# Projecting v for two groups of heads at once in a transformer layer on one core

## The chip, the core and the metric

The kernel runs on one core of a Trainium2 chip. A core has a matrix engine (TensorE, PE in the profile), a vector engine (VectorE, DVE), an engine for activations (ScalarE, ACT), a general one (GpSimd, POOL) and one that here only issues DMAs (SyncE, SP). They run their own instruction streams, each in order, and wait for each other by semaphores. The metric is device time in microseconds (us) of one execution. Before the change it is 2662.03 us in the median of three runs (2661.37 to 2664.33).

## What is computed

The input x has 8 batches of 1024 rows with 512 features. The reference, cut to its core:

```python
qkv = einsum('bte,fe->btf', layernorm(x), in_proj_weight).reshape(b, t, 3, 16, 32)
q, k, v = heads of qkv                      # 16 heads of 32 features
attn = softmax(causal(q @ k.T / sqrt(32)))  # per batch and head
x = x + (attn @ v) @ out_proj_weight.T
z = layernorm(x)                            # and then, over the 8 batches in order:
c = sigmoid(z@wf.T + c@uf.T + bf) * c + sigmoid(z@wi.T + c@ui.T + bi) * tanh(z@wc.T + c@uc.T + bc)
out = x + tanh(z @ wo.T + c_final @ uo.T + bo)
```

The recurrence runs over the batches, with 1024 rows at each step.

## The kernel before

**Numbers.** Matrices are split into two fp16 parts, a high and a low one, and a product is taken as three products of parts (high-high, high-low, low-high). A product over 512 features is therefore 3 x 4 = 12 matmuls into one PSUM buffer. The helper `three` (line 534) issues them with 512 moving columns each; all its matmuls stand under line 539 in the profile, told apart by their tiles.

**Groups.** The 16 heads of a batch are worked on in 4 groups of 4 heads, 32 groups over all batches; `s_` counts them, `b` is the batch and `g` the group in it. `proj(s_)` (line 547) projects a group:

- It loads three weight tiles (q, k, v; each 128 partitions x 2 parts x 4 x 128, 256 KB) from a DRAM tensor SQ. Their ring `wg` has three slots, which lie side by side in the raw tile wxr (so the profile calls them wxr). A ring hands out any free slot, and its users take their turn in order of creation (fifo).
- q and k: for each half of the 1024 rows, 12 matmuls with the weights stationary and 512 rows of zT (the normalized input, transposed) moving, into a buffer of the ring pj (two PSUM buffers). The moving operand is `zt()[:, :, c, k]`, four stretches of 128 columns that lie 2 KB apart. ScalarE (L570) and VectorE (L571) evict the high and low part into a tile `nat`, and a DMA writes it to DRAM (QK).
- v: here the rows are stationary and the weights move. For each half and each of its four blocks of 128 rows, 12 matmuls of 128 columns (line 586) write a quarter of one pj buffer. ScalarE (L591) and VectorE (L592) evict it, 128x512, into the one tile of ring `vs`, and a DMA writes that to DRAM (VD), 264 KB.

`stack_load` (line 600) later loads the stacked q and k into `stk` (three slots) and v into `vt`. `a_group` (line 637) computes scores for the row maxima in the PSUM buffer sa, `m_rows` (line 681) turns the maxima round with one matmul into sa (line 690) and copies them out on VectorE (line 692). `b_group` (line 759) and, from the 21st pair of heads on, `turned_rows` (line 729) compute scores again, exponentiate, split (GpSimd, line 757) and multiply by v (line 721). `out_proj` (line 855) projects the result; `recur` (line 882) runs the recurrence, with weights wf loaded from SF through a ring of two slots, and `csplit` (line 872) splits its state (lines 877 and 878).

**Order.** Nothing is issued by loops at run time. Every step is an operation with an engine, an estimated duration and a due time `at`; `Plan.schedule` (line 107) makes one fixed order from them before the program is built. At each step it takes the engine whose next operation can start earliest and, of those that can start at that moment, the one with the least due time. It counts with estimated durations (0.68 us for 12 matmuls of 128 columns), with ring slots that come free, and for a DMA with SP's time to issue it (0.32 us; 3.5 us for a transposing one), 270 GB/s on one common channel, and 2.2 us more to land. What comes out is each engine's instruction stream; on the chip an instruction that isn't ready holds up all behind it on its engine, SP's DMAs included.

Due times count in steps: one group has 65 (18 x TAU / 9 with TAU = 32.5). From a group's start, q is due at 0 and 5, k at 10 and 15, v at 20 and 25. On the chip a batch took 298 us around the middle of the run.

Of the kernel before, what the change touches and what calls it, by code (L numbers as in the profile page):

```python
# [10 lines left out]
F16 = mybir.dt.float16  # L11
# [23 lines left out]
class Ring:  # L35

    def __init__(self, tiles, fifo=True, over=()):
        self.tiles, self.fifo, self.over = tiles, fifo, over  # L40
        self.free = [(0.0, i) for i in range(len(tiles))]
        self.queue = deque()
        self.left, self.end = 0, 0.0

    def buf(self):
        return Buf(self)


class Buf:
    def __init__(self, ring=None, tile=None):  # L50
        self.ring, self.tile, self.slot = ring, tile, None
        self.left, self.end, self.acc = 0, 0.0, []
        self.view = None
        if ring is not None:
            ring.left += 1
            if ring.fifo:
                ring.queue.append(self)
# [19 lines left out]
class Plan:  # L77
# [29 lines left out]
    def schedule(self):  # L107
        avail = {e: [] for e in LATENCY}
        clock = {e: 0.0 for e in LATENCY}
        dma = 0.0  # L110

        shared = 0.0

        def enter(o):
            avail[o.eng].append(o)
            for e in o.alt:
                avail[e].append(o)

        for o in self.ops:
            o.n = len(o.pre)  # L120
            o.ready = 0.0
            for p in o.pre:
                p.succ.append(o)
            if not o.n:
                enter(o)
        left = len(self.ops)
        while left:
            best = None
            for e, l in avail.items():
                t = clock[e]  # L130
                pick = None
                for o in l:
                    s = o.ready if o.ready > t else t
                    if o.alt:

                        f = {x: max(o.ready, clock[x]) + y + SPARE.get(x, 0.0) for x, y in (*o.alt.items(), (o.eng, o.dur))}
                        if min(f.values()) < f[e]:
                            continue
                    if o.port and shared > s:
                        s = shared  # L140
                    if pick is not None and s > pick[0]:
                        continue
                    ok = True
                    for b in o.bufs:
                        if b.ring is not None and b.slot is None:
                            q = b.ring
                            if not q.free or (q.fifo and q.queue[0] is not b) or any(x.left for x in q.over):
                                ok = False
                                break
                            f = max([min(q.free)[0]] + [x.end for x in q.over])  # L150
                            if f > s:
                                s = f
                    if ok:
                        k = (s, o.at, o.seq)
                        if pick is None or k < pick[:3]:
                            pick = (*k, o)
                if pick is not None and (best is None or pick[0] < best[0]):
                    best = (*pick, e)
            assert best is not None, "the plan has no next operation"
            s, _, _, o, e = best  # L160
            avail[o.eng].remove(o)
            for x in o.alt:
                avail[x].remove(o)
            if e != o.eng:
                o.eng, o.dur = e, o.alt[e]
            for b in o.bufs:
                if b.ring is not None and b.slot is None:
                    x = min(b.ring.free)
                    b.ring.free.remove(x)
                    b.slot = x[1]  # L170
                    if b.ring.fifo:
                        b.ring.queue.popleft()
            o.start, o.end = s, s + o.dur
            clock[o.eng] = o.end
            if o.port:
                shared = o.end
            done = o.end + LATENCY[o.eng]
            if o.size is not None:
                dma = max(dma, o.end) + o.size / DMA_RATE
                done = dma + DMA_LATENCY  # L180
            for b in o.bufs:
                b.left -= 1
                b.end = max(b.end, done)
                if b.ring is not None and not b.left:
                    b.ring.free.append((b.end, b.slot))
                    b.ring.left -= 1
                    b.ring.end = max(b.ring.end, b.end)
            for x in o.succ:
                x.n -= 1
                x.ready = max(x.ready, o.end if x.eng == o.eng and o.size is None else done)  # L190
                if not x.n:
                    enter(x)
            left -= 1
        return sorted(self.ops, key=lambda o: (o.start, o.seq))
# [3 lines left out]
def layer(ctx, tc, x_in, wqkvT, woT, ffn, woffT, uoffT, vecs, bo, inc, out):  # L198
# [142 lines left out]
    def new(tag):  # L341
        return R[tag].buf()

    def dma(dst, src, at, r=(), w=(), size=256.0, hold=(), dur=0.32, transpose=False, after=(), e="SP"):

        if transpose:
            fn = lambda: sp.dma_start(dst(), src(), transpose=True)
        else:
            fn = lambda: eng[e].dma_start(dst(), src())
        return op(e, dur, fn, r, w, at, size * 1024.0, hold, after)  # L350
# [192 lines left out]


    wgs, QK, VD = {}, {}, {}

    def proj(s_):
        b, g = divmod(s_, G)
        at0 = t_a(18 * s_) - 1.7 * TAU - X_SH * max(0.0, 1 - s_ / X_RAMP) if s_ else -280.0
        for which in range(3):  # L550
            if (s_, which) not in wgs:
                w = wgs[s_, which] = new("wg")
                dma(w, lambda which=which: SQ()[g, which], at0 - 10.0 + 2 * PSTEP * which, r=[(SQ, (g, which))], w=[w])
        w = [wgs.pop((s_, i)) for i in range(3)]
        qk = QK[s_] = new("QK")
        vd = VD[s_] = new("VD")
        at = at0
        for which in range(2):
            t = new("nat")
            for half in range(2):  # L560
                if s_ == 0:
                    at = -250.0 + 60.0 * half
                zt, p = zT[b, half], new("pj")
                three(p, p, lambda c, k, zt=zt: zt()[:, :, c, k], lambda a, k, which=which: w[which]()[:, a, k], 512,
                      lambda k: [zt, w[which]], at)
                cols = slice(half * 512, half * 512 + 512)
                scale = 2.0 ** (-21 - which)
                hi = lambda t=t, cols=cols, which=which: t()[:, 1 - which, cols]
                lo = lambda t=t, cols=cols, which=which: t()[:, which, cols]
                op("ACT", 0.6, lambda p=p, hi=hi, scale=scale: act.activation(hi(), p(), AF.Copy, scale=scale), [p], [(t, (half, 0))], at)  # L570
                op("DVE", 0.7, lambda p=p, hi=hi, lo=lo, scale=scale: dve.scalar_tensor_tensor(lo(), p(), scale, hi(), ALU.mult, ALU.subtract),  # L571
                   [p, (t, (half, 0))], [(t, (half, 1))], at)
                at += PSTEP
            dma(lambda which=which: qk()[2 * which : 2 * which + 2].rearrange("w p t -> p w t"), t, at,
                r=[(t, (i, j)) for i in range(2) for j in range(2)], w=[(qk, which)], size=512)
        if s_ == 0:
            at = -100.0
        for half in range(2):
            v = new("vs")
            zt, p = zT[b, half], new("pj")  # L580
            for n in range(4):
                def fn(n=n, zt=zt, p=p):
                    i = 0
                    for k in range(KE):
                        for a, c in ((0, 0), (0, 1), (1, 0)):
                            pe.matmul(p()[:, n * 128 : n * 128 + 128], zt()[:, n, a, k], w[2]()[:, c, k], start=i == 0, stop=i == 3 * KE - 1)  # L586
                            i += 1
                op("PE", 0.68, fn, [(zt, n // 2) if b else (zt, (n // 2, n % 2)), w[2]], [p], at)
            src = lambda p=p: p().rearrange("p (n h d) -> p n h d", n=4, d=D)
            dst = v  # L590
            op("ACT", 0.6, lambda src=src, dst=dst: act.activation(dst()[:, :, :, 32:64], src(), AF.Copy, scale=2.0 ** -21), [p], [(v, 0)], at)  # L591
# [1 line left out]
               [p, (v, 0)], [(v, 1)], at)  # L593
            at += PSTEP
            dma(lambda half=half: vd()[:, half * 4 : half * 4 + 4], v, at, r=[(v, 0), (v, 1)], w=[(vd, half)], size=270)


    stk, vt, ms, MX = {}, {}, {}, {}

    def stack_load(P):  # L600
# [8 lines left out]
                at, r=[(qk, 0), (qk, 1)], w=[(t, j)])  # L609
        if p == 0:  # L610
            v = vt[s_] = new("vt")
            dma(v, VD[s_], t_b(9 * P) - 0.3 * TAU, r=[(VD[s_], 0), (VD[s_], 1)], w=[v], size=540)


    MASKED = 22
# [629 lines left out]
```

## Time and profile before

| | |
|---|---|
| median of three runs | 2662.03 us (2661.37 to 2664.33) |
| the profiled execution's own time | 2666.67 us |
| its span, first to last instruction | 2665.0 us |
| granted TensorE clock, mean | 0.996 |
| DMA moved | 477.99 MB, mean 179 GB/s |
| v projection, line 586 | 3072 matmuls, 219 ns for one (median) |
| its evictions, lines 591 and 592 | 597 and 686 ns for one (medians in batches five to eight) |
| weight tiles loaded from SQ | 93 DMAs, 3.3 us to landing (median) |
| v written to DRAM (VD<-vs) | 64 DMAs, 2.6 us to landing (median) |

How to read what follows. A row of the order of time has the start and the duration in us, engine, line, operation, tiles written <- read, shapes, and a count of like instructions merged; in brackets idle time of the engine before it and what ended it. The duration of one matmul holds its latency, and matmuls are pipelined, so what a matmul costs in a stream is read from the start of one row to the start of the next. A row of waits has the engine and line that waited, who was waited for, us in total, times, and the longest. "SPq" is SP's queue of DMA issues.

### The profile page before, as it was taken

The page shows a single profiled execution, that of the slowest core. Times are in us where ns is not written, and L with a number is a line of the kernel's source. Part 1 is how long each engine was busy: PE and PEld are TensorE (multiplying, and loading weights), DVE is VectorE, ACT ScalarE, POOL GpSimd, SP SyncE. Part 2 cuts the span into 40 slices and gives each one's busy share as a digit, 9 for nine tenths or more (in the row PEclk, how much of TensorE's full clock was granted, in tenths as well). Part 3 has the DMA queues.
Part 4 walks back from the last instruction along what each step waited for, and adds up shares of the span by engine and source line. Part 5 has one row for each costly group of instructions (what it writes and reads, how often), then busy time and mean ns, then how long its engine had stood idle before and what let it go on. Part 6 is the DMA issues. An engine that isn't in the chain of part 4 may idle for free.

```text
span 2665.0 us, 61520 instructions
## 1 busy us (share of the span) xinstructions
PE 2619.7 (98%) x24622; PEld 1512.8 (57%) x24636; DVE 1799.4 (68%) x4252; ACT 1836.3 (69%) x2290; POOL 1561.7 (59%) x1171
## 2 busy tenths in 40 slices
PE   8999999999999999999999999999999999999999
PEld 5666655666555555555555555555555555544444
DVE  5888777777677676767767676767776676422455
ACT  4688879888877777776777677777776777522222
POOL 3576777678667666666767666666766676400000
PEclk9999999999999999999999999999999999999999
DMA  6666676568567686687758686687756775564565
GB/s 228 172 194 196 157 185 173 147 173 217 134 148 187 187 203 164 171 201 177 195 148 191 182 207 165 171 195 193 185 145 161 187 172 128 148 205 150 197 223 211
DMA packets 526992, 477.99 MB, mean 179 GB/s; under 512 B 393841, under 2 KB 393841, under 8 KB 523121
## 3 DMA queue, kind: packets, MB, share of 16 engines
q1 hardware_dynamic: 526704, 474.06, 67.7%
q8 instruction: 193, 3.16, 0.5%
q14 instruction: 95, 0.77, 0.1%
HBM read 270.54 MB, written 108.53 MB: 142 GB/s over the span
## 4 chain that ended last, share of the span: by engine, by line
PE 87%; DVE 3%; DMA 2%; issue 1%; ACT 1%; POOL 0%; SPq 0%; DVEq 0%; ACTq 0%; POOLq 0%
PE pj L539 45%; PE av L721 9%; PE pt L539 8%; PE sb L779 7%; PE sa L665 7%; PE pj L586 5%; PE av L539 3%; PE sb L738 1%; DVE m L673 1%; DMA wf<-SF 1%; DVE cs L878 1%; PE sb L781 1%; PE sa L667 1%; DMA stkr<-mt 0%; ACT er L784 0%
## 5 line engine op out<-in xcount | busy, mean ns | idle before, releaser
L757 POOL TENSOR_TENSOR Pr<-er,Pr 128x1024 f16<-128x1024 f32 x569 | 1216.0, 2142 | 425.2 <-ACT Pr L756 330.8
L784 ACT ACTIVATE er<-sb,ebias,usc 128x1024 f32<-128x1024 f32 x488 | 586.2, 1201 | 175.2 <-PE sb L779 124.8
L539 PEld LDWEIGHTS <-wf 128*128 128x128 f16 x4320 | 401.3, 97 | 424.4 <-DMA wf<-SF 3.3
L756 ACT ACTIVATE Pr<-er 128x1024 f16<-128x1024 f32 x576 | 603.2, 1054 | 28.0 <-POOL er L793 17.5
L675 DVE CUSTOM_DVE_ANT_0 sa<-sa,tri 128x896 f32<-128x896 f32 (+3 forms) x588 | 409.8, 697 | 177.6 <-PE sa L665 167.1
L539 PE MATMUL pj<-z2T,wf 128*128 128x512 f16 x2016 | 497.6, 378 | 0.0
L539 PE MATMUL pj<-cs,wf 128*128 128x512 f16 x1728 | 419.8, 379 | 0.0
L721 PEld LDWEIGHTS <-Pr 128*128 128x128 f16 x9792 | 333.0, 96 | 84.5 <-issue 1.9
L539 PE MATMUL pj<-zT,wxr 128*128 128x512 f16 x1536 | 378.9, 380 | 0.2
L721 PE MATMUL av<-vt,Pr 128*128 128x65 f16 (+2 forms) x9792 | 348.5, 183 | 1.5 <-POOL Pr L757 0.9
L665 PE MATMUL sa<-stkr 96*128 96x512 f16 (+3 forms) x1348 | 299.2, 319 | 18.1 <-DVE m L673 10.2
L779 PE MATMUL sb<-stkr 98*128 98x128 f16 (+3 forms) x1624 | 308.6, 294 | 4.5 <-ACT er L784 2.4
L673 DVE TENSOR_REDUCE m<-sa 128x1 f32<-128x256 f32 (+7 forms) x340 | 241.3, 746 | 83.8 <-PE sa L667 83.1
L539 PEld LDWEIGHTS <-wxr 128*128 128x128 f16 x1728 | 158.8, 97 | 162.0 <-issue 2.6
L793 POOL TENSOR_SCALAR_AFFINE_SELECT er<-er 128x256 f32<-128x256 f32 (+1 forms) x336 | 122.1, 381 | 171.8 <-ACT er L784 169.1
L779 PEld LDWEIGHTS <-stkr 98*128 98x128 f16 x1624 | 143.1, 97 | 93.4 <-issue 3.6
L586 PE MATMUL pj<-wxr,zT 128*128 128x128 f16 x3072 | 194.2, 219 | 0.6 <-DVE C L911 0.6
L665 PEld LDWEIGHTS <-stkr 96*128 96x128 f16 x1360 | 120.7, 97 | 121.6 <-issue 22.9
L586 PEld LDWEIGHTS <-zT 128*128 128x128 f16 x3072 | 177.6, 98 | 11.1 <-issue 0.9
L539 PE MATMUL pj<-wo,aT 128*128 128x512 f16 x768 | 174.2, 379 | 0.2 <-DVE stkr L865 0.2
L459 POOL TENSOR_TENSOR zsr<-z,zsr 128x512 f16<-128x512 f32 x120 | 138.5, 1158 | 57.4 <-ACT zsr L458 55.5
L747 ACT ACTIVATE er<-sb,m,usc 128x1024 f32<-128x1024 f32 x88 | 105.8, 1202 | 82.0 <-DVE m L744 60.4
(186 smaller groups left out, 2888.7 us busy)
## 6 DMA issues: line engine op xcount, KB each, us to landing
wf<-SF SPq DMA_DIRECT2D x192, 512.0 KB, 3.9
stkr<-QK SPq DMA_DIRECT2D x192, 256.0 KB, 4.5
QK<-natr SPq DMA_DIRECT2D x64, 512.0 KB, 3.9
wxr<-x SPq DMA_DIRECT2D x112, 256.0 KB, 4.1
wxr<-SQ SPq DMA_DIRECT2D x93, 256.0 KB, 3.3
VD<-vs SPq DMA_DIRECT2D x64, 264.0 KB, 2.6
vt<-VD SPq DMA_DIRECT2D x32, 528.0 KB, 4.0
stkr<-X SPq DMA_DIRECT2D x16, 1024.0 KB, 7.3
```

Of the source, the lines that this page charges most:

```text
L459: o = op("DVE", 0.85, lambda: eng[o.eng].tensor_tensor(zs()[:, i, 1], z(), zs()[:, i, 0], ALU.subtract), [z, (zs, (i, 0))], [(zs, (i, 1))] ...
L539: pe.matmul(pv(), sv(a, k), mv_(b, k), start=first and k == 0 and i == 0, stop=last and k == KE - 1 and i == 2)
L586: pe.matmul(p()[:, n * 128 : n * 128 + 128], zt()[:, n, a, k], w[2]()[:, c, k], start=i == 0, stop=i == 3 * KE - 1)
L665: pe.matmul(pp()[:, lo:hi], q[:, h, qb * 128 : qb * 128 + 128], k[:, h, lo - off : hi - off], start=True, stop=not last, skip_group_check= ...
L673: dve.tensor_reduce(m()[:, h, qb : qb + 1], pp()[:, off : off + w], AX.X, ALU.max)
L675: dve.tensor_tensor_reduce(pp()[:, off : off + w], pp()[:, off : off + w], tri[:, T - w :], 1.0, NEG, ALU.add, ALU.max, m()[:, h, qb : qb ...
L721: pe.matmul(av()[:, o + z : o + z + y - x], stat(hl), v()[:, kb, i, x:y], start=c == 1, stop=c == total, skip_group_check=True)
L756: op("ACT", 1.06, lambda: act.activation(W()[:, 0], e(), AF.Copy), [e], [(W, 0)], at)
L757: lo = op("POOL", 2.18, lambda: eng[lo.eng].tensor_tensor(W()[:, 1], e(), W()[:, 0], ALU.subtract), [e, (W, 0)], [(W, 1)], at, alt={"DVE": ...
L779: pe.matmul(pp()[:, off : off + w], k[:, h, kb * 128 : kb * 128 + 128], q[:, h, qb0 * 128 : qb0 * 128 + w], start=True, stop=not last, ski ...
L784: op("ACT", 1.2, lambda: act.activation(e(), pp(), AF.Exp, bias=ebias, scale=TS), [pp, *s("TS")], [e], at)
L793: pool.affine_select(out=x, in_=x, pattern=[[0, n], [1, 128]], compare_op=ALU.is_ge, fill=0.0, base=0, channel_multiplier=-1)
```

## The change

From the fifth batch on (`TWO = 4`), v is projected only in even groups, for that group and the next together:

- An even group loads q's weights into slot 0 of `wg`, v's weights of its own and of the next group into slots 1 and 2, and k's weights into slot 0 again, once q's matmuls have freed it. An odd group loads q into slot 1 and k into slot 2. The slot wanted stands in a new field `want`, and the planner gives a buffer no other slot.
- `values` projects v: for a block of 128 rows, 12 matmuls with 256 moving columns (128 of each group, two stretches that lie 2 KB apart, read from slots 1 and 2 by one access pattern). Two blocks fill one pj buffer. Eviction by ScalarE and VectorE is of 128x512, as before. Two DMAs of half the size write one group's part each to DRAM.
- The four buffers of v in an even group are due at 20, 32, 44 and 56 from the group's start (`VSTEP = 12`). An odd group has q and k alone.

The first four batches, the attention, the recurrence and the end are as before. The diff, cut to its core:

```diff
+    def open(self, b):
+        return [f for f in self.free if b.want is None or f[1] == b.want]
...
-        self.view = None
+        self.view = self.want = None
...
-                            if not q.free or (q.fifo and q.queue[0] is not b) or any(x.left for x in q.over):
+                            free = q.open(b)
+                            if not free or (q.fifo and q.queue[0] is not b) or any(x.left for x in q.over):
...
+    VSTEP, VLATE = 12, 0
+    TWO = 4
...
-        for which in range(3):
+        two = b >= TWO and g % 2 == 0
+        loads = [(g, i) for i in range(3)] if b < TWO else [(g, 0), (g, 2), (g + 1, 2), (g, 1)] if two else [(g, 0), (g, 1)]
+        w = {}
+        for i, (gg, which) in enumerate(loads):
             if (s_, which) not in wgs:
-                w = wgs[s_, which] = new("wg")
-                dma(w, lambda which=which: SQ()[g, which], at0 - 10.0 + 2 * PSTEP * which, r=[(SQ, (g, which))], w=[w])
-        w = [wgs.pop((s_, i)) for i in range(3)]
+                x = new("wg")
+                if b >= TWO:
+                    x.want = (i if two else i + 1) % 3
+                dma(x, lambda gg=gg, which=which: SQ()[gg, which], at0 - 10.0 + 2 * PSTEP * min(i, 2), r=[(SQ, (gg, which))], w=[x])
+            else:
+                x = wgs.pop((s_, which))
+            w[which, gg] = x
...
+        if b >= TWO:
+            for half in range(2 if two else 0):
+                for m in range(2):
+                    values(s_, half, m, [w[2, g], w[2, g + 1]], at + VLATE)
+                    at += VSTEP
+            return
...
+    def values(s_, half, m, w, at):
+
+        v = new("vs")
+        zt, p = zT[s_ // G, half], new("pj")
+        for j in range(2):
+            def fn(n=2 * m + j, o=j * 256):
+                assert (w[0].slot, w[1].slot) == (1, 2)
+                ww = raw["wxr"][:, 512:1536].bitcast(F16).rearrange("p (g a k f) -> p g a k f", g=2, a=2, k=KE)
+                i = 0
+                for k in range(KE):
+                    for a, c in ((0, 0), (0, 1), (1, 0)):
+                        pe.matmul(p()[:, o : o + 256].rearrange("p (g f) -> p g f", g=2), zt()[:, n, a, k], ww[:, :, c, k], start=i == 0, stop=i == 3 * KE - 1)
+                        i += 1
+
+            op("PE", 1.32, fn, [(zt, m), *w], [p], at)
...
+        for i in range(2):
+            dma(lambda i=i: VD[s_ + i]()[:, half * 4 + 2 * m : half * 4 + 2 * m + 2].rearrange("p n h c -> p n (h c)"),
+                lambda i=i: v().rearrange("p (n g) h c -> p n g (h c)", g=2)[:, :, i], at + PSTEP, r=[(v, 0), (v, 1)], w=[(VD[s_ + i], (half, m))], size=135)
...
-            dma(v, VD[s_], t_b(9 * P) - 0.3 * TAU, r=[(VD[s_], 0), (VD[s_], 1)], w=[v], size=540)
+            dma(v, VD[s_], t_b(9 * P) - 0.3 * TAU, r=[VD[s_]], w=[v], size=540)
```

More of the change, by code (lines that the diff above doesn't have):

```diff
@@ L146, in schedule @@
                             q = b.ring
-                            if not q.free or (q.fifo and q.queue[0] is not b) or any(x.left for x in q.over):
+                            free = q.open(b)
+                            if not free or (q.fifo and q.queue[0] is not b) or any(x.left for x in q.over):
                                 ok = False
                                 break
-                            f = max([min(q.free)[0]] + [x.end for x in q.over])
+                            f = max([min(free)[0]] + [x.end for x in q.over])
                             if f > s:
@@ L167, in schedule @@
                 if b.ring is not None and b.slot is None:
-                    x = min(b.ring.free)
+                    x = min(b.ring.open(b))
                     b.ring.free.remove(x)
@@ L549, in proj @@
         at0 = t_a(18 * s_) - 1.7 * TAU - X_SH * max(0.0, 1 - s_ / X_RAMP) if s_ else -280.0
-        for which in range(3):
+        two = b >= TWO and g % 2 == 0
+        loads = [(g, i) for i in range(3)] if b < TWO else [(g, 0), (g, 2), (g + 1, 2), (g, 1)] if two else [(g, 0), (g, 1)]
+        w = {}
+        for i, (gg, which) in enumerate(loads):
             if (s_, which) not in wgs:
-                w = wgs[s_, which] = new("wg")
-                dma(w, lambda which=which: SQ()[g, which], at0 - 10.0 + 2 * PSTEP * which, r=[(SQ, (g, which))], w=[w])
-        w = [wgs.pop((s_, i)) for i in range(3)]
+                x = new("wg")
[5 more added lines that the diff above has]
+            w[which, gg] = x
         qk = QK[s_] = new("QK")
-        vd = VD[s_] = new("VD")
+        for i in range(2 if two else 0 if b >= TWO else 1):
+            VD[s_ + i] = new("VD")
+        vd = VD[s_]
         at = at0
@@ L563, in proj @@
                 zt, p = zT[b, half], new("pj")
-                three(p, p, lambda c, k, zt=zt: zt()[:, :, c, k], lambda a, k, which=which: w[which]()[:, a, k], 512,
-                      lambda k: [zt, w[which]], at)
+                three(p, p, lambda c, k, zt=zt: zt()[:, :, c, k], lambda a, k, which=which: w[which, g]()[:, a, k], 512,
+                      lambda k: [zt, w[which, g]], at)
                 cols = slice(half * 512, half * 512 + 512)
@@ L585, in fn @@
                         for a, c in ((0, 0), (0, 1), (1, 0)):
-                            pe.matmul(p()[:, n * 128 : n * 128 + 128], zt()[:, n, a, k], w[2]()[:, c, k], start=i == 0, stop=i == 3 * KE - 1)
+                            pe.matmul(p()[:, n * 128 : n * 128 + 128], zt()[:, n, a, k], w[2, g]()[:, c, k], start=i == 0, stop=i == 3 * KE - 1)
                             i += 1
-                op("PE", 0.68, fn, [(zt, n // 2) if b else (zt, (n // 2, n % 2)), w[2]], [p], at)
+                op("PE", 0.68, fn, [(zt, n // 2) if b else (zt, (n // 2, n % 2)), w[2, g]], [p], at)
             src = lambda p=p: p().rearrange("p (n h d) -> p n h d", n=4, d=D)
@@ L595, in proj @@
             dma(lambda half=half: vd()[:, half * 4 : half * 4 + 4], v, at, r=[(v, 0), (v, 1)], w=[(vd, half)], size=270)
+    def values(s_, half, m, w, at):
[11 more added lines that the diff above has]
+            op("PE", 1.32, fn, [(zt, m), *w], [p], at)
+        src = lambda: p().rearrange("p (n d) -> p n d", d=D)
+        dst = lambda: v().rearrange("p n h c -> p (n h) c")
+        op("ACT", 0.6, lambda: act.activation(dst()[:, :, 32:64], src(), AF.Copy, scale=2.0 ** -21), [p], [(v, 0)], at)
+        op("DVE", 0.7, lambda: dve.scalar_tensor_tensor(dst()[:, :, 0:32], src(), 2.0 ** -21, dst()[:, :, 32:64], ALU.mult, ALU.subtract),
+           [p, (v, 0)], [(v, 1)], at)
+        for i in range(2):
+            dma(lambda i=i: VD[s_ + i]()[:, half * 4 + 2 * m : half * 4 + 2 * m + 2].rearrange("p n h c -> p n (h c)"),
+                lambda i=i: v().rearrange("p (n g) h c -> p n g (h c)", g=2)[:, :, i], at + PSTEP, r=[(v, 0), (v, 1)], w=[(VD[s_ + i], (half, m))], size=135)
     stk, vt, ms, MX = {}, {}, {}, {}
```

## The prediction

> **What bounds the kernel now.** I read the page's table of busy time first, then its slices, then busy time by stretches of 100 us, then the waits of TensorE, then the order of time around the v projection.
>
> ```profile
> PE 2619.7 (98%) x24622; PEld 1512.8 (57%) x24636; DVE 1799.4 (68%) x4252; ACT 1836.3 (69%) x2290; POOL 1561.7 (59%) x1171
> ...
> PEclk9999999999999999999999999999999999999999
> ```
>
> TensorE is busy for 98% of the span at a full granted clock. No other engine comes near it. In busy time by stretches (start and end, length, busy time of PE, then the other engines), the batches that the change touches look like this:
>
> ```profile
> 1400.00:1500.00 100.00, 100.00 (x975) 59.56 (x974) 69.47 (x186) 73.03 (x90) 70.81 (x60) 1.00 0.83 198
> 1500.00:1600.00 100.00, 100.00 (x905) 56.62 (x903) 72.40 (x194) 74.08 (x95) 66.57 (x58) 1.00 0.78 191
> 1600.00:1700.00 100.00, 98.24 (x956) 57.27 (x953) 68.62 (x172) 74.09 (x90) 66.50 (x51) 1.00 0.66 157
> ```
>
> Most stretches have no idle time at all, and one in three lacks 1.76 us. So in this stage the time is the sum of what TensorE streams, plus one small wait a batch. From 1060 to 2200 us, which holds the v projections of the last four batches, TensorE's waits are two rows:
>
> ```profile
> PE sa L665 <- DVE mt L692: 7.0, 4, 1.8
> PE pj L586 <- DVE C L911: 0.6, 1, 0.6
> ```
>
> The change can therefore gain only what it takes from the stream, and these 7.6 us. It can lose whatever makes TensorE wait, because TensorE takes its instructions in a fixed order and nothing can overtake a matmul that waits.
>
> **The matmuls.** The last four batches hold 16 groups of four heads. Each group projects v with 96 matmuls of 128 columns, 1536 in all. The change makes 768 of 256 columns, with the same stationary tiles, each loaded half as often. What one costs is read from where the next row starts, since the duration of one (219 ns) is mostly latency:
>
> ```profile
> 1257.78 2.75 PE L539 MATMUL pj<-zT,wxr 128*128 128x512 f16 x12
> 1260.37 0.60 PE L665 MATMUL sa<-stkr 96*128 96x512 f16 x3
> ...
> 1273.36 2.17 PE L586 MATMUL pj<-wxr,zT 128*128 128x128 f16 x36
> 1275.37 0.60 PE L665 MATMUL sa<-stkr 96*128 96x512 f16 x3
> ```
>
> 36 matmuls of 128 columns take 1275.37 - 1273.36 = 2.01 us, 55.8 ns each. 12 of 512 columns take 1260.37 - 1257.78 = 2.59 us, 215.8 ns each. A straight line through both gives (215.8 - 55.8) / 384 = 0.417 ns a column and 2.4 ns for each matmul whatever its size. So 256 columns cost 55.8 + 128 x 0.417 = 109.2 ns. Two small ones cost 111.6 ns. The saving is 2.4 ns x 768 = **1.9 us**, which is all there is in the stream. The weight load (98 ns for one by itself) is already hidden: the matmuls of 128 columns follow each other in 55.8 ns, on the same line as the large ones, so halving the loads gives nothing.
>
> No matmul of 256 columns stands alone in a long run here, so I bound its cost. From below, half a matmul of 512 columns is 107.9 ns, a saving of 768 x 3.7 = 2.8 us. From above, 111.6 ns, a saving of nothing. A new matmul reads two stretches of 128 columns that lie 2 KB apart. The q and k projections read four stretches of 128 columns at that same step (line 564), and these are the very matmuls that take 215.8 ns, so a slower read is not to be expected. I take 1.9 us, nearest to both rows.
>
> [...]
>
> **The evictions.** Per pair of groups there were four evictions by ScalarE (L591, 597 ns) and four by VectorE (L592, 686 ns), each of 128x512, and there still are four of each. They cost nothing more. The two buffers of PSUM (pj) are taken as often and for as long (24 matmuls of 109.2 ns are 2.6 us, 48 of 55.8 ns were 2.7 us).
>
> **The DMAs.** The weight loads stay at six a pair of groups (four with the even group, two with the odd one). The writes of v to DRAM go from 32 to 64 of half the size; the row of these says 326 ns for an issue, so SP, which issues all DMAs in order, gets 32 x 0.33 = 10 us more in some 1100 us. SP spends most of its time waiting (the waits of its queue begin with 401.6 us behind line 539's matmuls), so I take nothing for it. The one staging tile (vs) is held until both writes land; a landing now takes 2.6 us in the median (2.1 to 5.3 in these batches) and the evictions are planned 12 us apart, so this is covered. Without that cover ScalarE would wait up to some 3 us, and behind it a PSUM buffer.
>
> **The new wait.** In an even group k's weights may only be loaded when q's slot is free. Nothing but q's second half stands between, and in half of these groups k follows q at once. In the 21st group the order of time has q's last three matmuls and k's first six in one unbroken row (counted from the group's start); below it are two rows of SP, and one of the page's table of DMAs (count, size, median us to landing).
>
> ```profile
> 1313.40 2.11 PE L539 MATMUL pj<-zT,wxr 128*128 128x512 f16 x9
> ...
> 1312.51 1.96 SPq L347 DMA_TRANSPOSE Pr<-Pr  x1
> 1316.62 0.35 SPq L349 DMA_DIRECT2D wxr<-SQ  x1
> ...
> wxr<-SQ SPq DMA_DIRECT2D x93, 256.0 KB, 3.3
> ```
>
> The load into that very slot (for the next group, today) was issued at 1316.62, some 2.5 us after q's three (1313.40 + 3 x 0.216 = 1314.05), because SP was behind a transpose; with 3.3 us to landing, k's weights would be there nearly 6 us after q. If k stayed where it is in the order, TensorE would stand for that long with attention and recurrence queued behind it. But the order is not fixed by hand: the planner gives a load 256 KB / 270 GB/s + 2.2 us plus SP's own time, and puts other ready matmuls first. In the odd group q's and k's slots come free only after the last v matmul. By the due times that v is planned at 56 and the next q at 65, and its weights need 2.6 us of matmuls and some 4 us of load, so 2 to 3 us are spare.
>
> How good such planning is can be read from the same kernel. The recurrence's weights (wf<-SF, 192 loads of 512 KB, 3.9 us to landing) also go through a ring of two and are also loaded when a slot is freed. TensorE waited for them three times, 1.8 us in all, and never in the stretch above. So I take 0 for 8 loads of k and 8 pairs of the odd groups, with bounds of 0 and 8 x 3.3 = 26 us (a whole landing for each of k's loads). Against a gain from it speaks that weights never made TensorE wait here.
>
> **The small wait.** The 7.0 us are four waits of 1.76 us, one a batch, at 1080, 1378, 1676 and 1975 us, beside the q projection of the second group:
>
> ```profile
> 1372.86 5.22 DVE L878 SCALAR_TENSOR_TENSOR cs<-C,sig,cs 128x512 f16<-128x512 f32 x2
> 1378.00 0.27 DVE L692 CAST mt<-sa 32x128 f16<-32x128 f32 x1
> ...
> 1378.33 0.59 PE L665 MATMUL sa<-stkr 96*128 96x512 f16 x3 [1.76 <-DVE mt L692]
> ```
>
> VectorE's two operations took 5.22 us in place of twice 0.7 while GpSimd ran; the copy from the score buffer came late, and the next scores with it. It is an accident of alignment, and the change moves 2.6-us blocks of v to just ahead of this place. It may go, stay, or come twice. I take it as unchanged, with bounds of -7.0 us and +7.0 us.
>
> **The sum.** -1.9 (stream) + 0 (weights) + 0 (alignment) = -1.9 us. The profiled execution took 2666.67 us with a span of 2665.0; by the sum it becomes 2664.8. The median of the runs is 2662.03, 4.6 lower, and with the same step it becomes **2660 us**.
>
> **The rivals.**
> 1. The alignment resolves. All four waits of line 665 go: -1.9 - 7.0 = -8.9, 2653 us. For it: batches two to four (480 to 1060 us) show only 0.6 us of waits. Against it: the cause (VectorE behind GpSimd) stays.
> 2. Slower: k's weights come late in the even groups. It decides from (5.3 + 1.9) / 8 = 0.9 us a load on, where the loss leaves the band of 0.2%. For it: SP's order is fixed too, and it was 2.5 us late for this slot; the slowest landing of these tiles was 8.5 us. Against it: the recurrence's loads. With a landing exposed in the four groups where k follows q at once: 4 x 3.3 - 1.9 = +11.3, 2673 us; in all eight, 26.4 - 1.9, 2686 us.
> 3. The change doesn't do what it says: the wide matmul streams no faster than two, 2662 us.
>
> **How the numbers follow.** The likeliest case has 0.55 (own range 2657 to 2667), the first rival 0.2, the second 0.2, the third 0.05. A measurement of this kernel can tell about 0.2%, 5.3 us, from no change: below 2656.7 is faster, above 2667.4 slower. Faster gets the first rival's 0.2, slower the second's 0.2, the same 0.6. The range reaches from just under the first rival, 2652, to just over the second's first price, 2675; what is left out is eight full landings, or waits that pile up at several places.
>
> **What would show it.** In the profile after: 768 matmuls of 256 columns that follow each other in about 109 ns, and 1536 of 128 columns left; TensorE busy about 2 us less. In its waits, line 539 behind a DMA of wxr from SQ would show the second rival, and the row of line 665 behind line 692 missing or doubled decides the first. I am wrong if TensorE's busy time falls by 10 us or more (the loads did count), or if its idle time from 1060 to 2200 us leaves 0 to 15 us.

## The result and the profile after

The changed kernel takes 2684.37 us in the median of five runs (2682.87 to 2687.51), the kernel before 2663.39 us beside it (2661.37 to 2668.21): a ratio of 1.0078, with a 95% interval of 1.0064 to 1.0092. It is **21 us slower**. The prediction said 2660 us, a range up to 2675, and gave slower 2 in 10.

The profiled execution took 2687.51 us with a span of 2685.8. The page's first line on it:

```profile
PE 2628.2 (98%) x23868; PEld 1503.1 (56%) x23868; DVE 1819.6 (68%) x4249; ACT 1834.3 (68%) x2290; POOL 1565.5 (58%) x1174
```

In fewer matmuls TensorE is busy for 8.5 us more, and the span has grown by 20.8. Up to about 940 us both executions keep pace; what differs is the part that the change touches. Busy time in the same kind of stretch as before (the number after the five engines is the granted clock, 0.98 in one of the two and 1.00 in both before):

```profile
1400.00:1500.00 100.00, 97.91 (x809) 53.43 (x808) 66.16 (x179) 71.16 (x90) 68.31 (x58) 0.98 0.72 183
1500.00:1600.00 100.00, 99.38 (x872) 56.61 (x869) 72.89 (x188) 71.47 (x91) 65.99 (x58) 1.00 0.73 193
```

Before, two stretches in three had no idle time at all; now each has some. The four largest rows of TensorE's waits from 980 to 2260 us name what it lacks (three more have 1.3 us together):

```profile
PE pj L544 <- DVE C L966: 12.4, 13, 2.1
PE av L768 <- POOL Pr L804: 2.7, 2, 1.7
PE pj L544 <- DVE natr L588: 1.6, 4, 0.4
PE pj L544 <- DVE C L958: 1.3, 3, 0.4
```

(Lines have moved. Matmuls: 544 is the old 539, 712 the old 665, 737 the old 690, 768 the old 721, 785 the old 738, 631 the new v. On VectorE: 958 is the old 911, 965 and 966 are the old 918 and 919, 588 the old 571. On GpSimd: 804 is the old 757.) Twenty waits, 15.3 us, are for a buffer of `pj`: a matmul waits for VectorE to empty one of the two PSUM buffers that projections, recurrence and output projection share. Before, the same stretch had one such row, 0.6 us. The 7.0 us of line 665 behind line 692 are gone, and no wait is for weights from SQ. The longest of these waits, in order of time, TensorE first and then VectorE:

```profile
1444.15 0.81 PE L544 MATMUL pj<-zT,wxr 128*128 128x512 f16 x3
...
1445.68 0.60 PE L768 MATMUL av<-vt,Pr 128*128 128x65 f16 x16
1448.36 1.10 PE L544 MATMUL pj<-z2T,wf 128*128 128x512 f16 x3 [2.09 <-DVE C L966]
1449.25 1.06 PE L785 MATMUL sb<-stkr 96*128 96x512 f16 x2
...
1446.85 0.73 DVE L965 SCALAR_TENSOR_TENSOR pj<-pj,g 128x512 f32<-128x512 f32 x1
1447.61 0.69 DVE L966 SCALAR_TENSOR_TENSOR C<-pj,C 128x512 f32<-128x512 f32 x1
1448.22 0.68 DVE L588 SCALAR_TENSOR_TENSOR natr<-pj,natr 128x512 f16<-128x512 f32 x1
```

One buffer holds a recurrence unit, the other the first half of q, which the new order has taken early: nine of its twelve matmuls ran from 1433.08 on, the last three only at 1444.15, so it holds its buffer for nearly 16 us, until 1448.90. VectorE empties both only from 1446.85 on. For 2.09 us TensorE takes up no matmul. What follows is slow: the two matmuls of 512 columns from 1449.25 to 1450.10 take 0.43 us each in place of 0.216. In busy time by stretches:

```profile
1440.00:1448.30 8.30, 6.27 (x65) 3.78 (x64) 6.39 (x20) 7.53 (x11) 6.12 (x5) 1.00 0.94 210
1448.30:1452.30 4.00, 3.94 (x25) 1.89 (x25) 2.57 (x6) 1.32 (x2) 2.83 (x4) 0.57 1.08 227
1452.30:1460.00 7.70, 7.70 (x68) 4.12 (x67) 3.13 (x7) 2.00 (x2) 3.11 (x2) 1.00 0.64 117
```

The granted clock is 0.57 for these 4 us, which is 3.4 us at one half, and 1.00 on both sides. Slow matmuls count as busy (3.94 of these 4.00 us), which raises the busy time.

**The account of one batch.** Around the middle of the run both executions repeat with the batch: before from 1378.33 to 1676.40 us, 298.07 us; after from 1448.36 to 1751.65 us, 303.29 us. The difference is 5.22. I took each matmul's distance to the start of the next one, less 0.417 ns a column and 2.4 ns, as its excess (for a wait it comes out some 0.16 us larger than the idle time in the profile's rows: 1.92 for 1.76):

| us in one batch | before | after |
|---|---|---|
| longest wait for pj | 0 | 2.24 |
| half clock behind it | 0 | 1.6 |
| four shorter waits for pj | 0 | 2.61 |
| four excesses of about 0.28 each | 0 | 1.14 |
| wait of line 665 for the copy (line 692) | 1.92 | 0 |
| 192 wide matmuls for 384 narrow ones | 0 | -0.46 |

The sum of after less before is 5.2. The four batches are not quite alike: at the same matmul of the recurrence, a batch apart, the changed kernel is behind by 3.5, 8.7, 13.9 and 21.2 us (0.8 ahead before them). The first has no stretch at half clock and loses less, the last loses more. The same excess over all of 980 to 2260 us (what is above 0.1 us, and all at half clock) gives the whole loss:

| us from 980 to 2260 us | before | after |
|---|---|---|
| ahead of a matmul into pj | 0.8 | 18.7 |
| at half clock | 0 | 4.6 |
| ahead of one into sa | 7.7 | 5.1 |
| ahead of one into av or sb | 0.2 | 3.8 |

That is 23.4 us more; less 1.8 us for 768 wide matmuls in place of 1536, it is 21.6.

### The profile page after: what moved, and what is told of

It is laid out like the page before. It is cut to its first block, busy times and chain, and to the rows that moved or that the text cites. A ratio compares the mean times of both kernels' runs of the same rounds, so it can differ in the third digit from the quotient of the medians.

```text
span 2685.8 us, 59995 instructions
## 1 busy us (share of the span) xinstructions
PE 2628.2 (98%) x23868; PEld 1503.1 (56%) x23868; DVE 1819.6 (68%) x4249; ACT 1834.3 (68%) x2290; POOL 1565.5 (58%) x1174
## 4 chain that ended last, share of the span: by engine, by line
PE 54%; DVE 4%; DMA 1%; issue 0%; ACT 0%; POOL 0%; DVEq 0%; ACTq 0%
PE pj L544 28%; PE pt L544 8%; PE av L768 4%; PE sb L826 3%; PE sa L712 3%; PE av L544 3%; PE pj L631 2%; PE sb L785 1%; DVE mh L735 1%; DVE sa L722 1%; DVE sb L790 1%; DVE cs L925 0%; DMA wf<-SF 0%; DVE C L966 0%; DVE pj L965 0%
## 5 line engine op out<-in xcount | busy, mean ns | idle before, releaser
L544 PE MATMUL pj<-z2T,wf 128*128 128x512 f16 x2016 | 505.1, 380 | 11.7 <-DVE C L966 10.5
L712 PE MATMUL sa<-stkr 96*128 96x512 f16 (+3 forms) x1348 | 299.3, 319 | 12.1 <-DVE m L720 10.0
L790 DVE CUSTOM_DVE_ANT_0 sb<-sb,tri 128x1024 f32<-128x1024 f32 x88 | 109.0, 1239 | 84.2 <-PE sb L785 78.2
L451 POOL TENSOR_TENSOR rs<-rs,nhalf 128x1 f32<-128x1 f32 x120 | 71.2, 595 | 116.4 <-DVE rs L448 90.8
```

The lines of the kernel that those rows point to most:

```text
L544: pe.matmul(pv(), sv(a, k), mv_(b, k), start=first and k == 0 and i == 0, stop=last and k == KE - 1 and i == 2)
L712: pe.matmul(pp()[:, lo:hi], q[:, h, qb * 128 : qb * 128 + 128], k[:, h, lo - off : hi - off], start=True, stop=not last, skip_group_check= ...
L790: dve.tensor_tensor_reduce(pp(), pp(), tri, 1.0, NEG, ALU.add, ALU.max, m1()[:, 0:1])
```

## The experiments

Theory 1 is that moving v in the due times gave an order in which TensorE waits for PSUM buffers. Theory 2 is that k's late weights cost it, theory 3 that the wide matmul does. Ratios are to the kernel before on the same chip; its medians there were 2664.5 to 2665.3 us.

**1. The change with narrow matmuls, same order.**

```diff
-                        pe.matmul(p()[:, o : o + 256].rearrange("p (g f) -> p g f", g=2), zt()[:, n, a, k], ww[:, :, c, k], start=i == 0, stop=i == 3 * KE - 1)
+                for g in range(2):
...
+                            pe.matmul(p()[:, o + g * 128 : o + g * 128 + 128], zt()[:, n, a, k], ww[:, g, c, k], start=i == 0, stop=i == 3 * KE - 1)
```

> The changed kernel with its order, slots and loads untouched (the planner still counts 1.32 us for 24 matmuls), but v by 1536 matmuls of 128 columns in place of 768 of 256. Theory 1 (the order: moved due times make TensorE wait for PSUM buffers, width is a small gain): 1 to 3 us slower than the changed kernel, about 2686 us, with the same waits for pj. Theory 2 (late weights of k): the same 2686. Theory 3 (the wide matmul itself costs): back to about 2663 to 2670 us.

Measured 2685.82 us, 1.0082 (1.0065 to 1.01): as slow as the change, with the same rows of waits (12.1 us behind the recurrence's update in place of 12.4). Theory 3 is out.

**2. The slots and k's late load alone.**

```diff
-        for which in range(3):
+        for which in (0, 2, 1) if b >= 4 and g % 2 == 0 else range(3):
...
+                    w.want = (1 if which == 2 else 0) if g % 2 == 0 else (2, 0, 1)[which]
```

> The kernel before, with the slots of the change alone: from the fifth batch on, an even group loads q into slot 0, v into slot 1 and k into slot 0 once q's matmuls have freed it; an odd group loads q, k, v into slots 2, 0, 1. v stays narrow and where it was. The planner's own finishing time goes up by 5 us. Theory 1: 3 to 8 us slower than before, through the order, and no wait of TensorE for a landing of k's weights. Theory 2: nearly all of the 21 us, with rows of line 541 behind a DMA of wxr. Theory 3: no change.

Measured 2664.67 us, 0.9994 (0.9985 to 1.0004): no difference. The 3 to 8 us that theory 1 gave it did not come either. Theory 2 is out for k. (The odd groups' slots are not the change's here, so their loads are not tested by this run; that no wait of the changed kernel is for weights from SQ covers them.) All its waits from 980 to 2260 us; none is for a landing of weights:

```profile
PE pj L543 <- DVE natr L577: 2.2, 5, 0.9
PE sa L671 <- DVE mt L698: 1.8, 1, 1.8
PE sa L671 <- DVE m L681: 0.7, 3, 0.2
PE pj L592 <- DVE C L917: 0.6, 1, 0.6
```

**3. The kernel before, with v due 10 later.**

```diff
+        at += 10 if b >= 4 else 0
         for half in range(2):
             v = new("vs")
```

> The kernel before, with one number changed: from the fifth batch on, v is due 10 later (30 and 35 from the group's start in place of 20 and 25). No wide matmul, no shared weights, no late load. The planner's own finishing time goes up by 17 us (for the change it goes up by 18). Theory 1: 12 to 22 us slower than before, about 2680 us, by waits of TensorE for PSUM buffers and for attention tiles that were not there before. Theories 2 and 3: no change, 2661 to 2667 us.

Measured 2674.63 us, 1.0039 (1.0025 to 1.0053): 9 us slower from one due time alone, less than the 12 to 22 expected. So the order costs something by itself, with nothing of the change's work in it. The two largest rows of TensorE's waits in the same stretch; the first is of the kind that the change has, the second is one wait for the score buffer:

```profile
PE pj L539 <- DVE C L920: 3.3, 4, 0.9
PE sa L666 <- DVE m L676: 2.3, 2, 2.0
```

All six rows sum to 8.4 us, hardly more than the 7.6 before, for many of the new waits are too short for a row. By the excess of the matmuls the delays from 980 to 2260 us are 14.9 us in place of 8.7: 5.8 for pj in place of 0.8, 7.5 for sa in place of 7.7, and 1.6 for av.

**4. The change with other due times.** They were chosen by the planner's own finishing time.

```diff
-    VSTEP, VLATE = 12, 0
+    VSTEP, VLATE = 14, -5
...
+        at0 -= 10.0 if b >= TWO and not two else 0.0
```

> The changed kernel with three other due times: v of an even group due at 15, 29, 43 and 57 (in place of 20, 32, 44, 56), and everything of an odd group 10 earlier. Wide matmul, shared slots and k's late load are kept. The planner's own finishing time falls to that of the kernel before (2704.0 against 2704.2). Theory 1: 2658 to 2666 us, level with before. Theories 2 and 3: about 2684 us, as the change.

Measured 2673.92 us, 1.0033 (1.0021 to 1.0045). Three due times give back more than half of the loss, which no theory but the first allows, though not all of it, which I had expected. The largest part of what is left stands in the first row of its waits from 980 to 2260 us, which the plan does not have:

```profile
PE pj L544 <- DVE natr L589: 7.8, 4, 1.9
```

In order of time, VectorE and then TensorE:

```profile
1382.01 3.22 DVE L926 SCALAR_TENSOR_TENSOR cs<-C,sig,cs 128x512 f16<-128x512 f32 x2
1385.15 0.68 DVE L589 SCALAR_TENSOR_TENSOR natr<-pj,natr 128x512 f16<-128x512 f32 x1
...
1385.88 4.44 PE L544 MATMUL pj<-zT,wxr 128*128 128x512 f16 x12 [1.94 <-DVE natr L589]
```

Two splits of the state took 3.22 us on VectorE in place of twice 0.74, and the eviction behind them came late. It is the kind of accident that cost 1.76 us a batch before the change, near the same place of the batch, now on another waiter.

**5. The change with three PSUM buffers for pj.** One bank moves from av to pj; due times, slots and work stay. (The ring pt, which the last batch's recurrence uses, contains av's buffers and so has one fewer too.) The planner makes a new order for it, over the whole run.

```diff
-        "pj": ring("pj", 2, [128, 512], F32, False, ps),
+        "pj": ring("pj", 3, [128, 512], F32, False, ps),
...
-        "av": ring("av", 2, [128, 512], F32, True, ps),
+        "av": ring("av", 1, [128, 512], F32, True, ps),
```

> The changed kernel with one PSUM bank moved: three buffers for the projections and the recurrence (pj) in place of two, one for the products with v (av) in place of two. Due times, slots, loads and the wide matmul are the change's. Theory 1a (the 21 us are waits for one of two PSUM buffers, which the moved due times bunch up): most of it comes back, 2660 to 2670 us, and the rows of TensorE waiting for a pj buffer behind VectorE shrink from 15 us to under 4. Rival 1b (TensorE lacks ready work at these places whatever the buffers, since VectorE and GpSimd are late): 2678 us or more, the waits move to av, sa or sb.

Measured 2664.11 us, 1.0000 (0.9991 to 1.001): all of the 21 us are back. All waits of TensorE from 980 to 2260 us:

```profile
PE pj L544 <- DVE wxr L912: 1.0, 1, 1.0
PE av L768 <- DVE os L891: 0.7, 2, 0.4
PE sa L712 <- DVE m L722: 0.3, 1, 0.3
```

The excess there is 5.9 us in place of the change's 32.1, of it 1.2 for pj. Rival 1b, that the waits would only move to other buffers, is out for this part of the run. The profile is of the slowest of the eleven runs (2671.59 us): from the same matmul of the recurrence at about 2250 us to the end it takes 13 us longer than the kernel before, where the other profiles with three buffers differ by 3 us at most.

**6. The kernel before with three.** The same two lines in the kernel before.

> The kernel before with the same bank moved (three pj, one av). The planner's own finishing time falls by 6 us. Theory 1a: little to gain, since TensorE has 7.6 us of waits there in the last four batches and waits for pj are hardly among them: 2655 to 2664 us. Rival 1b: 2663 us, or slower by what one av buffer costs.

Measured 2664.92 us, 1.0001 (0.9992 to 1.001). The third buffer gives nothing where no one waits for it, and one av buffer costs nothing that the time shows (1.2 us of waits for it from 980 to 2260 us); the 6 us that the planner saw did not come.

**7. Filling the long wait.** Each filler runs only when sa is free, which leaves part of the wait idle.

```diff
+        if o.eng == "PE":
+            if 900.0 < o.start < 2300.0 and o.start - busy > 2.0:
+                idle(R["sa"].tiles[0], 2048)
...
+            busy = o.end
```

> The changed kernel with four matmuls of 512 columns without use (0.86 us) added at each of the four places where the plan leaves TensorE idle for over 2 us, into the score buffer sa, which is free there. The order of all else is the same. If the half clock after these idle stretches (three stretches of 3.4 us at 0.5 in the profile) comes from the idleness, it goes, and the time falls by about 1.7 us at each, 4 to 6 us in all, to 2679 us. If it doesn't come from there, the time stays at 2684 us or rises by up to 2.

Measured 2679.63 us, 1.0051 (1.0035 to 1.0066), 5 us less than the change's median; the two intervals just touch. The half clock behind these waits is gone; two of the three stretches of 100 us that showed 0.98 are printed here, the clock is 1.00 in all three:

```profile
1400.00:1500.00 100.00, 98.94 (x868) 54.75 (x865) 67.53 (x186) 72.31 (x92) 69.38 (x60) 1.00 0.77 187
1700.00:1800.00 100.00, 98.94 (x838) 54.25 (x837) 67.77 (x186) 72.19 (x90) 69.54 (x60) 1.00 0.74 190
```

One other stretch of half clock stands in this profile, at 1006.57 us, behind two waits that got no filler (1.01 and 0.86 us). So about a quarter of the loss was not the waits but the clock after them, and work without use takes it back.

**8. A version that beats both, and whose merit it is.** The first kernel is the change with three pj buffers as in experiment 5 and due times chosen again:

```diff
-    VSTEP, VLATE = 12, 0
+    VSTEP, VLATE = 14, 0
...
+        at0 += (2.0 if two else -5.0) if b >= TWO else 0.0
...
+            at += 10.0 if which and b >= TWO else 0.0
```

> The changed kernel with three pj and one av buffer and other due times from the fifth batch on (v of an even group every 14, k 10 later, even groups 2 later, odd ones 5 earlier); the planner's own finishing time is 10 us under that of the kernel before. Theory 1a: 2653 to 2661 us, faster than both. Rival 1b: 2665 us or more.

Measured 2659.69 us, 0.9979 (0.997 to 0.9988), and once more on another chip, beside two controls. One has narrow matmuls as in experiment 1. The other is the kernel before with three pj buffers and these due times:

```diff
+        at0 += (5.0 if g % 2 == 0 else -10.0) if b >= 4 else 0.0
...
+            at += 5.0 if which and b >= 4 else 0.0
...
+        at += 5.0 if b >= 4 else 0.0
...
-            at += PSTEP
+            at += 20.0 if b >= 4 else PSTEP
```

> The retimed changed kernel with three pj buffers, as it was, on the same chip as the two controls: 2657 to 2662 us.

> The retimed kernel with three pj buffers (2659.7 us), its order untouched, but with two matmuls of 128 columns for each of 256. Theory 1 (a wide matmul saves 2.4 ns, 1.9 us in all): 2660 to 2664 us, 1 to 3 us above the retimed kernel on this chip. If the wide matmul is worth more once nothing waits: over 5 us above it.

> The kernel before with three pj and one av buffer, v narrow and unpaired, and due times from the fifth batch on that were looked for in the same way (v due 5 later and its second half 20 after the first, k 5 later, even groups 5 later, odd ones 10 earlier); the planner's own finishing time is 1 us above that of the retimed changed kernel. If the 5 us that the retimed kernel gained come from buffers and due times: 2658 to 2663 us, as that one and 1 to 3 us above it. If they come from pairing v: 2664 us or more.

The retimed kernel: 2659.96 us, 0.9981 (0.9972 to 0.999). The same order with narrow matmuls: 2658.97 us, 0.998 (0.9971 to 0.9989). The kernel before, v unpaired and narrow, with three buffers and due times searched in the same way: **2657.26 us, 0.9976** (0.9965 to 0.9987). From 980 to 2260 us its profile has no row of TensorE waiting at all. All three lie within each other's intervals. The gain over the kernel before comes from buffers and due times together; neither pairing v nor the wide matmul has a part in it that these runs can tell.

## Why the prediction was wrong

**What held.** TensorE sets the time (busy for 98% of the span before and after), and the stream was priced right: twelve wide matmuls take 1368.34 - 1367.02 = 1.32 us in the changed kernel, 110 ns each where 109.2 were expected.

```profile
1367.02 1.48 PE L631 MATMUL pj<-wxr,zT 128*128 128x256 f16 x12
1368.34 0.60 PE L712 MATMUL sa<-stkr 96*128 96x512 f16 x3
```

That the hidden weight loads give nothing also held: wide and narrow in one order differ by less than the runs' scatter, twice (1.0082 narrow to the change's 1.0078 in experiment 1, 0.998 to 0.9981 in experiment 8). The 1.9 us of the stream are too few for the times to tell. The late weights of k cost nothing, as taken (experiment 2, 0.9994). The small wait of line 692 did go, as the first rival had it.

**What failed** is the step on the evictions: "The two buffers of PSUM (pj) are taken as often and for as long." As a count and as an average it was right, though the 2.6 us given for it are matmuls alone: from the first matmul into a buffer to the end of VectorE's last read, v's 32 uses in the stretch from 980 to 2260 us last 6.47 us in the mean before and 6.45 after, and the two buffers are held for 71% of it before and 72% after. But I let the average stand for the wait, and put the wait at nothing; it measured 18.7 us in place of 0.8, with 4.6 us at half clock behind waits. Which two outputs hold the buffers at one time, and when VectorE comes to empty them, is set by the order, and the change made a new order. I priced the moved due times only where an old wait stood (the alignment, 0 with bounds of 7 us either way) and nowhere for waits that the profile before did not yet have. With every stretch at 100.00, the profile showed that the cover was complete, not that there was any to spare: the planner's greedy order had fitted two buffers without a gap, and the change's due times no longer did.

The slower rival was the wrong mechanism as well: weights from DRAM, not buffers of PSUM. The prediction's own sign, 0 to 15 us of idle time from 1060 to 2200 us, was passed: the rows there sum to 16.7 us. A range for "any new order makes TensorE wait" was missing. Experiments 2, 3 and 4 show its size: nothing, +9 us for one due time, and 10 us between two settings of the same work. And the plan had told it: with the change its finishing time rises by 18 us, and it leaves TensorE idle for over 2 us at four places (experiment 7). A plan is made before the program runs, so the prediction could have read this from it.

**What stays open.** The planner's finishing time had the change right (18 us above the kernel before, measured 21), but it missed others by 5 to 9 us (experiments 2, 3, 4 and 6: +5, +17, 0 and -6 planned, -1, +9, +9 and 0 measured). Experiment 5 gave the planner a third buffer and with it a new order from the start of the run, so it shows what the buffer is worth to the planner, not to one fixed order. Of the four excesses of 0.28 us a batch, three are waits of the matmul that turns the row maxima (line 737) for VectorE's line 735 just before it, which took 2.1 us there and 0.16 at the least; they are no waits for pj, and why they come with this order was not followed.

## What to carry to other kernels

When an engine is at 100% and its order is made by a planner, price a change of due times as a new order: look for the resource with the fewest slots that several streams share (here two PSUM buffers for three users), and read the planner's finishing time and its idle stretches before and after. It can miss, but zero is no safe price: new orders of the same work cost 21, 9 and 0 us here. Test it by giving that resource one slot more before blaming the moved work. A gain of 1.9 us in the stream is undone by a single wait of 2 us.

## What the runs showed of the hardware

**The granted clock was one half behind some short waits.** Behind a wait of 2.09 us (the changed kernel) TensorE ran at half clock for 3.4 us in two of three cases, behind 1.94 us (experiment 4) in two of four, behind 1.76 us (the kernel before) in none of four. Behind two waits close together it was seen too: 1.66 and 0.86 us in the changed kernel but not in experiment 1, 1.01 and 0.86 us in experiments 1 and 7 but not in the changed kernel and experiment 4. So waits of 2 us were at times enough in these runs. What decides between such cases was not tested.

**VectorE's split was slow beside GpSimd's subtraction.** From 960 to 2260 us in the kernel before, the state's split (line 878) has a median of 0.74 us and a longest of 2.69. The nine splits that ran beside GpSimd's subtraction (line 757, 2.1 us for one) for over 2 us took 2.61 to 2.69 each; eight that ran beside it for 0.28 to 0.33 us took 0.74. In the 5.22 us pair the two took 2.68 and 2.61, while line 757 ran from 1370.78 to 1375.00 and again from 1375.33 on. The durations show that it went with the overlap; why was not tested. The planner lets no two operations with its mark `port` run at one time, and both lines have the mark, but on the chip the two met.
